# Layer 0 of a graph network: one-hot products among half-array ones as two of 64 columns, lists loaded by SP, a pause before each fetched block

## The chip, the cores and the metric

The kernel runs on one core of a Trainium2 chip. The core has a matrix engine (TensorE, PE in the profile; its weight loads are PEld), a vector engine (VectorE, DVE), a scalar engine (ScalarE, ACT), a general engine (GpSimd, POOL), and a sequencer that issues transfers (SyncE, SP), beside 16 DMA engines that all queues share. Each engine works through its own instructions in order and waits on semaphores for the others. The metric is the device time of one execution in microseconds, lower is better.

## The reference

The input is a graph of 12500 nodes with 64 features and 212500 directed edges, sorted by their receiving node (`dst`), each with 64 features of its own. What is computed, cut to what matters:

```python
h = maximum(layernorm(x), 0)
for i in range(3):                                   # layers 0, 1, 2
    agg = segment_sum(h[src], dst) / maximum(count(dst), 1)
    h = agg @ Wl[i] + h @ Wr[i] + b[i]               # relu after all but the last
x = x + h
h = maximum(layernorm(x), 0)
agg = segment_sum(edge_attr, dst) / maximum(count(dst), 1)
y = relu(concat(agg, h) @ W0 + b0); y = relu(y @ W1 + b1)
out = x + y @ W2 + b2
```

## The kernel before

Nodes stand in 98 blocks of 128. The sum over the edges of a node is computed in two ways.

**Dense blocks (78 of 98, in 20 groups of four, the last of two).** For each group the kernel builds a matrix of counts, 12544 x 512 bytes of fp8: how often each source node sends to each receiver. A layer multiplies the rows of h with it. The rows stand as three bf16 parts side by side (3 x 64 columns), whose sum is the f32 value. `Layer.group` does it in two streams of 98 products with 512 moving columns each: `whole` (line 392) takes two of the parts as 128 columns of the array; `half` (line 403) takes the third part as 64 columns, even blocks of nodes into the lower half of the array's columns and of the accumulator's partitions, odd ones into the upper. `Weave.run` orders them: 56 whole products, 56 half ones, the other 42 whole ones, the other 42 half ones.

**Fetched blocks (the first 20 of 98).** Here each block takes 19 x 128 edges in order. For each 128 edges GpSimd gathers the rows of h by an indirect DMA (`fetch`, line 461, tile `got`, eight tiles, so eight fetches ahead), and one product of 128 columns with a one-hot matrix of the receivers' places (`own`, made by VectorE in `mark`) adds them up in the accumulator `pg` (`use`, line 489). Two blocks share one accumulator; VectorE reduces it into `ga` (line 496) before the next two may use it. `use(i)` also requests fetch i + 8.

**Weave.** All other work is hung between these streams. `wide(pos, fn)` puts a function behind the whole product number `pos` of a layer (1960 of them, the position); `narrow(pos, sub, fn)` puts one behind half product `sub` of a group. `spread` places the 380 products of the fetched blocks at positions `spot(i, first)`: evenly spaced from `first` (220, 90 and 60 in layers 0, 1 and 2) to 90 before the end.

**Layer 0 also builds the matrices.** During the stream of group t, matrix t + 1 is built. VectorE makes one-hot operands (`h` with L790 and L791, `c` with L792) in batches of 8 or 10 of them; `pair` (line 809) multiplies two of them into an accumulator `pb`, 128 columns with 245 moving, and ScalarE casts that to the matrix (L812). There are three such accumulators. Of the 26 pairs of two blocks, or 52 of a group, 40 stand at positions among the whole products and 12 are `narrow`, two at a time, at half products 6, 20, 34, 48, 62 and 76. SP stores each half of a matrix to DRAM when its last cast is done (line 834); layers 1 and 2 load them back.

What goes into the one-hots comes from `index(j, box)`: a search for the first edge of each node of four blocks. It is a chain over the engines, each step hung at an offset: ScalarE counts the heads of tiles that lie before the node (0), GpSimd gathers the tile of 512 receivers, `ends` (7), ScalarE counts in it, `inside` (29), VectorE works out the edge and GpSimd gathers 128 receivers and senders from there, `to` and `of` (36, line 567), and so on. `coded(t)` hangs that for matrix t at 15 before the end of a group. `listed(j)` does the same for the five sets of four fetched blocks, and appends `lists(j)`: eight gathers on GpSimd, two for each block (108 and 120), of the receivers and senders of its 19 x 128 edges, then VectorE's working-out of places and rows (150). It begins 255 positions before the set's first product (205 for the first set).

The orders on TensorE, VectorE, ScalarE and GpSimd are those of the code; SP's follows a scheduler. In layers 1 and 2 SP also loads blocks of edge features: `load` reads the first edge into a register (`values_load`) and issues a plain load from there.

Of the kernel before, what the change touches and what calls it, by code (L numbers as in the profile page):

```python
# [11 lines left out]
F32 = mybir.dt.float32  # L12
I32 = mybir.dt.int32
# [6 lines left out]
ALU = mybir.AluOpType  # L20
# [9 lines left out]
P = 128  # L30
# [41 lines left out]
def in_order(  # L72
# [196 lines left out]
    class Carved:  # L269
# [6 lines left out]
        def tile(self, shape, dtype, name, bufs=None):  # L276
            size = 1
            for k in shape[1:]:
                size *= k
            if name not in self.places:  # L280
                self.places[name] = self.at
                self.at += self.bufs * size
            k = self.uses[name] = self.uses.get(name, -1) + 1
            o = self.places[name] + k % self.bufs * size
            t = self.t[: shape[0], o : o + size]
            return t if len(shape) == 2 else t.rearrange("p (a d) -> p a d", d=shape[2])
# [7 lines left out]
    class Weave:  # L294
# [2 lines left out]

        def __init__(self):
            self.w, self.seq, self.wides, self.narrows = 0, 0, [], []

        def wide(self, pos, fn):
            self.seq += 1
# [6 lines left out]
        def run(self, whole, half):  # L309


            half = enumerate(half)
            for n in (TURN, None):
                for _ in islice(whole, n):
                    self.w += 1
                    while self.wides and self.wides[0][0] <= self.w:
                        heapq.heappop(self.wides)[2]()
                for i, _ in islice(half, n):
                    due = [f for f in self.narrows if f[0] <= i and f[1] <= self.w]
                    for f in sorted(due):  # L320
                        self.narrows.remove(f)
                        f[3]()
                    heapq.heapify(self.narrows)

        def rest(self):
            while self.wides or self.narrows:
# [29 lines left out]
    class Layer:  # L356
# [122 lines left out]
        def use(self, i):  # L479
            b, k = divmod(i, EK)  # L480
            if i == 0:
                self.mark(0, 0)
            if i % (2 * EK) == 0:
                self.pg = self.psg.tile([P, 2, 3 * D], F32, name="pg")
            if i % (4 * EK) == 0:
                self.ga = self.pool.tile([P, 4, D], F32, name="ga", bufs=2)
            if k % QE == 0:
                self.mark(b, k // QE + 1)
            nc.tensor.matmul(  # L489
                self.pg[:, b % 2, :], self.owned.pop(i), self.fetched.pop(i),  # L490
                start=k == 0, stop=k == EK - 1,
            )
            self.fetch(i + NGOT)
            if k + 1 < EK:
                return
            nc.vector.tensor_reduce(  # L496
                self.ga[:, b % 4, :],
                self.pg[:, b % 2, :].rearrange("p (i d) -> p d i", i=3), axis=AX.X, op=ALU.add,
            )
            if b % 4 == 3:  # L500
                ga, j0, w = self.ga, b - 3, self.weave
                box = {}

                def sums():
                    pt = self.psc.tile([D, 4, P], F32, name="pt")
                    for k in range(4):
                        nc.tensor.transpose(pt[:, k, :], ga[:, k, :], ident)
                    box["agg"] = self.pool.tile([D, 4 * P], F32, name="gat", bufs=1)
                    nc.scalar.copy(box["agg"], pt.rearrange("p k n -> p (k n)"))

                def own_rows():
                    ht = self.turn(j0, 4)
                    w.wide(w.w + 9, lambda: self.mix(box["agg"], ht, j0, 4, inv_u))

                w.narrow(w.w + 1, 40, sums)
                w.narrow(w.w + 1, 68, own_rows)

    steps = NB * len(dense_groups)

    def spot(i, first):  # L520

        return first + i * (steps - first - 90) / (EK * GB)

    def spread(layer, first):
        for i in range(EK * GB):
# [18 lines left out]
    with ExitStack() as s:  # L544
# [27 lines left out]
        def index(j, box):  # L572
# [17 lines left out]
            def ends():  # L590

                box["tile"] = tile("tile_of", 1)
                nc.vector.tensor_scalar(
                    box["tile"], box["s"], -0.5, 1.0 - TT / 2, op0=ALU.mult, op1=ALU.max
                )
                tile_i = tile("tile_i", 1, I32)
                nc.vector.tensor_scalar(tile_i, box["tile"], TT / 2 - 1.0, None, op0=ALU.add)
                box["ends"] = tile("ends", TW, I32)
                gather(box["ends"], tiles_d, tile_i[:, :1])

            def inside():
# [130 lines left out]
        def lists(j):  # L732

            box = {}

            def edges(k0):
                if k0 == 0:
                    box["of"] = idx.tile([P, 4, EK], I32, name="l_of")
                    box["to"] = idx.tile([P, 4, EK], I32, name="l_to")
                for k in (k0, k0 + 1):  # L740
                    b = 4 * j + k
                    gather(box["to"][:, k, :], dst, mine[:, b : b + 1])
                    gather(box["of"][:, k, :], src, mine[:, b : b + 1])

            def places():
                for k in range(4):
                    b = 4 * j + k
                    nc.vector.tensor_scalar(
                        place[:, b], box["to"][:, k, :, None].to_broadcast([P, EK, 2]),
                        float(b * P), None, op0=ALU.subtract,  # L750
                    )
                lo = idx.tile([P, 4, EK], I32, name="l_lo")
                nc.vector.tensor_scalar(lo, box["of"], P - 1, None, op0=ALU.bitwise_and)
                hi = idx.tile([P, 4, EK], I32, name="l_hi")
                nc.vector.tensor_scalar(hi, box["of"], 7, None, op0=ALU.logical_shift_right)
                nc.vector.scalar_tensor_tensor(
                    rows_of[:, 4 * j : 4 * j + 4, :], lo, float(NB), hi, op0=ALU.mult, op1=ALU.add
                )

            return [(108, lambda: edges(0)), (120, lambda: edges(2)), (150, places)]  # L760
# [38 lines left out]
        def build(m, t, n):  # L799


            def pair(block, q):
                for i, (t_, k, q0, _) in enumerate(batches):
                    if (t_, k, q0) == (t, block, q):
                        hots(i + 1 + AHEAD)
                pb = ps_b.tile([P, 2, 256], F32, name="pb")
                for i in range(2):
                    h, c = ready.pop((t, block, q + i))
                    nc.tensor.matmul(pb[:, i, : HP * WD], h, c, start=True, stop=True)  # L809
                k = WD if q < Q5 else WD - 1  # L810
                o = P * (block % 2) + WD * q - max(q - Q5, 0)
                nc.scalar.copy(  # L812
                    m[:, block // 2, :, o : o + 2 * k].rearrange("p h (w d) -> p h w d", d=k),
                    pb[:, :, : HP * WD].rearrange("p w (h d) -> p h w d", d=WD)[:, :, :, :k],
                )

            return [
                lambda b=b, q=q: pair(b, q) for b in range(n) for q in range(0, QW, 2)
            ]
# [103 lines left out]
        with tc.manual_schedule(engines={PE, DVE, ACT, POOL}):  # L923
# [34 lines left out]
                    w.wide(at + a, f)  # L958

            for j in range(GB // 4):  # L960
                steps_at(spot(4 * EK * j, FIRST) - (255 if j else 205), listed(j))
            w.wide(FIRST - 50, layer.fetch_first)
            spread(layer, FIRST)
            steps_at(1 - 15, coded(2))
# [55 lines left out]
    def load(b):  # L1020
        if b is None:
            return

        n = EK * P
        raw = ed.tile([P, n // P * D + 1], F32, name="raw")
        first = raw[:1, n // P * D :].bitcast(I32)
        nc.vector.tensor_scalar(first, mine[:1, b : b + 1], float(EP - n), None, op0=ALU.min)
        at0 = nc.values_load(
            first, engines=[SP], min_val=0, max_val=EP - n,
            skip_runtime_bounds_check_because="it is clamped, and is not under 0",  # L1030
        )
        raw = raw[:, : n // P * D].rearrange("p (k d) -> p k d", d=D)
        nc.sync.dma_start(raw, edge[ds(at0, n), :].rearrange("(p k) d -> p k d", k=EK))
        if b < GB:
            box[b] = raw, place[:, b]
            return
        to = ed.tile([P, EK], I32, name="e_to")
        nc.sync.dma_start(to, dst[ds(at0, n), :].rearrange("(p k) o -> p (k o)", k=EK))
        at = ed.tile([P, EK, 2], BF16, name="e_at")
        nc.vector.tensor_scalar(  # L1040
            at, to[:, :, None].to_broadcast([P, EK, 2]), float(b * P), None, op0=ALU.subtract
        )
        box[b] = raw, at
# [734 lines left out]
```

## Time and profile before

| what | value |
|---|---|
| time, median of 3 runs (lowest to highest) | 2887.91 us (2884.1 to 2899.18) |
| the profiled execution, its time | 2895.6 us |
| its span, first to last instruction | 2893.7 us |
| mean clock granted to TensorE | 0.985 |
| setup, to the first product of group 0 | 0 to 94 us |
| layer 0 | 94 to 1124 us |
| layer 1 | 1124 to 1876 us |
| layer 2 with edge sums and the last perceptron | 1876 us to the end |
| L392, L403 (whole, half products) | 1960 of each in each layer |
| L809 (one-hot products of the build) | 2028, all before 1091 us |
| L489 (products of fetched blocks) | 380 in each layer |

Layers are told apart by the first and the last of their products on L392. The time of a run includes some 2 us around the span. A product's duration in the profile is longer than its share of the stream, since products are pipelined: L392 has a mean of 378 ns, but one begins 0.216 us after the other. What a product costs is therefore read from one start to the next.

### The profile page before, as it was taken

To read this page: it belongs to the slowest core of one execution; us is meant where nothing else is said; L and a number is where in the kernel's file an instruction comes from. 1 tells how busy PE (TensorE), PEld (TensorE's weight loads), DVE (VectorE), ACT (ScalarE), POOL (GpSimd) and SP (SyncE) were. 2 spreads that over 40 slices of the span, in tenths; PEclk is the share of its full clock that TensorE was granted. 3 is DMA by queue.
4 is the path that set the end of the run, shared out by engine and by line. 5 is a ranking of instruction groups with operands and counts; after the bars stand their busy time and mean duration, and the time that the engine had idled before them with its cause. 6 is when DMAs were issued, how large, how long until landed. Compare 5 with 4: busy or idle time off the path is not lost.

```text
span 2893.7 us, 50078 instructions
## 1 busy us (share of the span) xinstructions
PE 2749.0 (95%) x19505; PEld 1600.9 (55%) x19505; DVE 1630.9 (56%) x3376; ACT 1122.5 (39%) x2339; POOL 1429.8 (49%) x1313
## 2 busy tenths in 40 slices
PE   1699999999999998999999999999999999999997
PEld 0455555555555554555555555655656565565655
DVE  8878788788788771211111111166666566666663
ACT  4666566666666661100000000033333333434332
POOL 5345667667575640555555555244444344444440
PEclk9999999999999998999999999999999999999998
DMA  3334434444444346766656665577667676667661
GB/s 97 160 128 169 154 137 169 169 164 149 160 167 156 138 158 224 236 212 210 208 190 205 210 212 191 191 232 238 218 200 226 195 231 216 203 219 232 207 211 36
DMA packets 203194, 537.43 MB, mean 186 GB/s; under 512 B 83874, under 2 KB 92195, under 8 KB 197955
## 3 DMA queue, kind: packets, MB, share of 16 engines
q1 hardware_dynamic: 143890, 458.08, 44.2%
q0 software_dynamic: 41360, 66.33, 10.2%
q10 hardware_dynamic: 17696, 9.74, 1.1%
q8 instruction: 154, 2.52, 0.4%
q14 instruction: 94, 0.76, 0.1%
HBM read 391.11 MB, written 142.90 MB: 185 GB/s over the span
## 4 chain that ended last, share of the span: by engine, by line
PE 83%; DVE 12%; DMA 3%; issue 1%; ACT 1%; POOL 0%; SPq 0%; ACTq 0%; DVEq 0%; POOLq 0%
PE p L392 39%; PE p L403 21%; PE pb L809 6%; PE pe L1138 5%; PE pg L489 3%; DVE c L792 3%; PE po L436 3%; PE po L440 3%; DVE h L790 2%; PE pt L425 2%; DVE h L791 1%; PE pm L1177 1%; PE pm L1186 1%; DMA ends<-in_dst_dram,tile_i 1%; DMA e_to<-in_dst_dram 1%
## 5 line engine op out<-in xcount | busy, mean ns | idle before, releaser
L461 POOL DMA_INDIRECT got<-h_d,rows_of x1140 | 1244.2, 1091 | 1246.0 <-PE pg L489 881.0
L812 ACT CAST m<-pb 128x490 uint16<-128x490 f32 (+1 forms) x1014 | 545.7, 564 | 329.1 <-PE pb L809 318.4
L392 PE MATMUL p<-m,rows 128*128 128x512 fp8e3 (+1 forms) x1960 | 569.6, 378 | 0.8 <-ACT m L812 0.8
L392 PEld LDWEIGHTS <-rows 128*128 128x128 bf16 x3920 | 374.6, 100 | 245.6 <-issue 45.9
L392 PE MATMUL p<-t,rows 128*128 128x512 fp8e3 (+1 forms) x1960 | 491.8, 378 | 0.9 <-ACT rows L263 0.9
L392 PE MATMUL p<-t,m 128*128 128x512 fp8e3 (+1 forms) x1960 | 458.4, 376 | 0.0
L809 PE MATMUL pb<-c,h 128*128 128x245 bf16 x2028 | 371.2, 276 | 57.0 <-ACT m L812 42.0
L336 DVE TENSOR_TENSOR own<-iota_l,place 128x640 bf16<-128x640 bf16 (+3 forms) x280 | 144.2, 516 | 360.2 <-PE pg L489 337.0
L403 PEld LDWEIGHTS <-rows 128*64 128x64 bf16 x3920 | 224.9, 110 | 217.5 <-issue 79.1
L809 PEld LDWEIGHTS <-h 128*128 128x128 bf16 x2028 | 190.9, 99 | 263.4 <-issue 105.5
L792 DVE TENSOR_TENSOR c<-iota_c,col 128x1968 bf16<-128x1968 bf16 (+1 forms) x234 | 298.6, 1276 | 0.0
L489 PE MATMUL pg<-got,own 128*128 128x192 bf16 x1140 | 281.7, 247 | 15.7 <-DVE ga L496 8.3
L392 PEld LDWEIGHTS <-m 128*128 128x128 bf16 x1960 | 184.7, 99 | 184.0 <-issue 13.9
L403 PE MATMUL p<-m,rows 128*64 128x512 fp8e3 (+1 forms) x1960 | 254.1, 378 | 0.0
L403 PE MATMUL p<-t,rows 128*64 128x512 fp8e3 (+1 forms) x1960 | 252.0, 377 | 0.0
L1052 ACT CAST cut<-raw 128x640 bf16<-128x640 f32 x196 | 136.5, 697 | 247.7 <-PE pe L1138 221.6
L790 DVE TENSOR_TENSOR h<-iota_l,lo 128x1024 bf16<-128x1024 bf16 (+1 forms) x234 | 173.6, 742 | 94.9 <-PE pb L809 94.4
L403 PE MATMUL p<-t,m 128*64 128x512 fp8e3 (+1 forms) x1960 | 225.5, 375 | 0.0
L1054 ACT CAST cut<-e_rest 128x640 bf16<-128x640 f32 x196 | 136.8, 698 | 221.5 <-DVE e_rest L1053 220.5
L1055 DVE TENSOR_TENSOR cut<-e_rest,cut 128x640 bf16<-128x640 f32 x196 | 154.8, 790 | 81.9 <-ACT cut L1054 81.4
L1138 PE MATMUL pe<-cut,own 128*128 128x192 bf16 x1862 | 188.3, 248 | 0.0
L1138 PEld LDWEIGHTS <-own 128*128 128x128 bf16 x1862 | 161.6, 99 | 40.5 <-issue 2.9
(189 smaller groups left out, 2566.1 us busy)
## 6 DMA issues: line engine op xcount, KB each, us to landing
t<-mat SPq DMA_DIRECT2D x546, 448.0 KB, 5.9
mat<-m SPq DMA_DIRECT2D x39, 3136.0 KB, 9.9
raw<-in_edge_dram SPq DMA_DIRECT2D x98, 608.0 KB, 4.1
got<-h_d,rows_of POOLq DMA_INDIRECT x1140
h_d<-rows SPq DMA_DIRECT2D x14, 336.0 KB, 2.2
h_d<-rows ACTq DMA_DIRECT2D x24, 192.0 KB, 2.5
h_d<-out SPq DMA_DIRECT2D x21, 192.0 KB, 1.9
m<-h_d SPq DMA_DIRECT2D x6, 576.0 KB
```

The lines of the kernel that those rows point to most:

```text
L336: nc.vector.tensor_tensor(t[:, :n].rearrange("p k (c t) -> p k c t", t=2), iota_l.rearrange("p (c t) -> p c t", t=2)[:, None].to_broadcast ...
L392: nc.tensor.matmul(p1, rows[:, i, : 2 * D], at(i), start=i == 0, stop=i == NB - 1)
L403: nc.tensor.matmul(p2[h], rows[:, i, 2 * D :], at(i), start=i < 2, stop=i >= NB - 2)
L461: nc.gpsimd.indirect_dma_start(out=t, out_offset=None, in_=h_rows[self.l], in_offset=bass.IndirectOffsetOnAxis(ap=rows_of[:, b, k : k + 1] ...
L489: nc.tensor.matmul(self.pg[:, b % 2, :], self.owned.pop(i), self.fetched.pop(i), start=k == 0, stop=k == EK - 1,)
L790: nc.vector.tensor_tensor(split(th), pairs(iota_l, P), own(lo, P), op=ALU.is_equal)
L792: nc.vector.tensor_tensor(split(tc_), pairs(iota_c, CW), own(col, CW), op=ALU.is_equal)
L809: nc.tensor.matmul(pb[:, i, : HP * WD], h, c, start=True, stop=True)
L812: nc.scalar.copy(m[:, block // 2, :, o : o + 2 * k].rearrange("p h (w d) -> p h w d", d=k), pb[:, :, : HP * WD].rearrange("p w (h d) -> p ...
L1054: nc.scalar.copy(c[:, :, D : 2 * D], rest)
L1055: nc.vector.tensor_tensor(c[:, :, 2 * D :], rest, c[:, :, D : 2 * D], op=ALU.subtract)
L1138: nc.tensor.matmul(box["pe"], o[:, k - k0, :], c[:, k - k0, :], start=k == 0, stop=k == EK - 1)
```

## The change

Three things change.

1. `Weave` keeps a flag `halved`, which is true while half products are issued. A new method `product` issues a product as two of 64 columns each, with the same moving operand, into the lower and the upper 64 partitions of the accumulator, while the flag is true, and as one of 128 otherwise. `use` and `pair` issue theirs through it. Functions hung by `wide` run while the flag is false, so it is the 12 pairs of each of 19 matrices hung by `narrow` that are split: 456 products become 912. Layers 1 and 2 have none.
2. The lists of the fetched blocks no longer go by gathers on GpSimd. VectorE clamps the first edges of four blocks (`l_at`), SP reads each into a register, and two plain loads of 128 x 19 words fetch receivers and senders. The `ends` tile of `index` has one buffer instead of two. `first_of` and `in_block` are the shared helpers; `load` of the edge features uses them too and does what it did.
3. `spot` places the gathered products by 21 slots for each block of 19, the first two of them empty. This holds for all three layers. `listed(0)` begins 215 instead of 205 before its first product.

```diff
@@ class Weave
+            self.halved = False
...
             for n in (TURN, None):
+                self.halved = False
                 for _ in islice(whole, n):
                     self.w += 1
...
+                self.halved = True
                 for i, _ in islice(half, n):
...
+            self.halved = False
+
+        def product(self, out, lhsT, rhs, start, stop):
+
+            for h in (slice(0, D), slice(D, P)) if self.halved else (slice(0, P),):
+                nc.tensor.matmul(out[h], lhsT[:, h], rhs, start=start, stop=stop)
@@ Layer.use
-            nc.tensor.matmul(
+            self.weave.product(
                 self.pg[:, b % 2, :], self.owned.pop(i), self.fetched.pop(i),
-                start=k == 0, stop=k == EK - 1,
+                k == 0, k == EK - 1,
             )
@@
+    def first_of(at):
+        return nc.values_load(
+            at, engines=[SP], min_val=0, max_val=EP - EK * P,
+            skip_runtime_bounds_check_because="it is clamped, and is not under 0",
+        )
+
+    def in_block(table, at0):
+        return table[ds(at0, EK * P), :].rearrange("(p k) d -> p (k d)", k=EK)
+
     def spot(i, first):
 
-        return first + i * (steps - first - 90) / (EK * GB)
+        b, k = divmod(i, EK)
+        return first + (b * (EK + 2) + k + 2) * (steps - first - 90) / ((EK + 2) * GB)
@@ index
-                box["ends"] = tile("ends", TW, I32)
+                box["ends"] = tile("ends", TW, I32, 1)
                 gather(box["ends"], tiles_d, tile_i[:, :1])
@@ lists
                     box["to"] = idx.tile([P, 4, EK], I32, name="l_to")
+                    box["at"] = idx.tile([1, 4], I32, name="l_at", bufs=2)
+                    nc.vector.tensor_scalar(
+                        box["at"], mine[:1, 4 * j : 4 * j + 4], float(EP - EK * P), None,
+                        op0=ALU.min,
+                    )
                 for k in (k0, k0 + 1):
-                    b = 4 * j + k
-                    gather(box["to"][:, k, :], dst, mine[:, b : b + 1])
-                    gather(box["of"][:, k, :], src, mine[:, b : b + 1])
+                    at0 = first_of(box["at"][:, k : k + 1])
+                    for to, ends in ((box["to"], dst), (box["of"], src)):
+                        nc.sync.dma_start(to[:, k, :], in_block(ends, at0))
@@ pair
-                    nc.tensor.matmul(pb[:, i, : HP * WD], h, c, start=True, stop=True)
+                    layer.weave.product(pb[:, i, : HP * WD], h, c, True, True)
@@
-                steps_at(spot(4 * EK * j, FIRST) - (255 if j else 205), listed(j))
+                steps_at(spot(4 * EK * j, FIRST) - (255 if j else 215), listed(j))
```

More of the change, by code (lines that the diff above doesn't have):

```diff
@@ L1022, in load @@
             return
[L1024 to L1033, printed above, removed]
+        raw = ed.tile([P, EK * D + 1], F32, name="raw")
+        first = raw[:1, EK * D :].bitcast(I32)
+        nc.vector.tensor_scalar(first, mine[:1, b : b + 1], float(EP - EK * P), None, op0=ALU.min)
+        at0 = first_of(first)
+        nc.sync.dma_start(raw[:, : EK * D], in_block(edge, at0))
+        raw = raw[:, : EK * D].rearrange("p (k d) -> p k d", d=D)
         if b < GB:
@@ L1037, in load @@
         to = ed.tile([P, EK], I32, name="e_to")
[L1038 removed]
+        nc.sync.dma_start(to, in_block(dst, at0))
         at = ed.tile([P, EK, 2], BF16, name="e_at")
```

## The prediction

> **What bounds the kernel now.** I read the page's head and the table of slices first, then the busy time of each engine by layer, then TensorE's waits in layer 0, then the timeline of one group of layer 0, and last the waits of GpSimd there.
>
> ```profile
> span 2893.7 us, 50078 instructions
> PE 2749.0 (95%) x19505; PEld 1600.9 (55%) x19505; DVE 1630.9 (56%) x3376; ACT 1122.5 (39%) x2339; POOL 1429.8 (49%) x1313
> DVE  8878788788788771211111111166666566666663
> PE 83%; DVE 12%; DMA 3%; issue 1%; ACT 1%; POOL 0%; SPq 0%; ACTq 0%; DVEq 0%; POOLq 0%
> ```
>
> TensorE (PE) is busy 95% of the span and carries 83% of the chain that ended last. The slices of VectorE (DVE) show where another engine comes near: the first 15 or so, layer 0, at eight tenths. By layer (columns: stretch, its length, busy of PE, PEld, DVE, ACT, POOL with instruction counts, clock, DMA share, GB/s):
>
> ```profile
> 94.00:1124.00 1030.00, 994.33 (x7075) 578.97 (x7074) 802.30 (x1652) 645.23 (x1457) 593.34 (x494) 0.99 0.44 161
> 1124.00:1876.00 752.00, 741.05 (x5063) 406.26 (x5063) 110.93 (x253) 54.25 (x108) 363.06 (x380) 0.99 0.63 207
> 1876.00:2894.00 1018.00, 996.98 (x7303) 606.19 (x7297) 632.74 (x1275) 376.99 (x663) 425.12 (x380) 0.98 0.65 205
> ```
>
> In layer 0 VectorE still has 1030 - 802 = 228 us idle and GpSimd 437 us, so a shorter TensorE stream there shortens the layer. What TensorE loses to waits in layer 0 (total us, times, longest) is little:
>
> ```profile
> PE po L436 <- DVE e L409: 11.7, 13, 3.9
> PE pb L809 <- ACT m L812: 11.0, 12, 5.6
> PE pg L489 <- DVE ga L496: 5.1, 4, 2.0
> PE pg L489 <- DVE own L336: 3.1, 1, 3.1
> PE pg L489 <- DMA got<-h_d,rows_of: 3.1, 2, 1.6
> ```
>
> A larger loss is no wait. The timeline around 401 us (start, length, instruction, count) shows half-array products (128*64, L403) with one-hot products (128*128, L809) among them:
>
> ```profile
> 401.26 0.84 PE L403 MATMUL p<-m,rows 128*64 128x512 fp8e3 x6
> 402.03 0.60 PE L809 MATMUL pb<-c,h 128*128 128x245 bf16 x4
> 402.56 0.84 PE L403 MATMUL p<-m,rows 128*64 128x512 fp8e3 x6
> ...
> 405.40 2.56 PE L403 MATMUL p<-m,rows 128*64 128x512 fp8e3 x21
> ```
>
> The 21 products at 405.40 are ten and a half pairs in 2.56 us: a pair takes 0.216 us, as its second half starts 0.004 us after the first in the records of the trace. So three pairs from 401.26 should end streaming at 401.91, but L809 starts at 402.03; four products at 0.105 should take 0.42 us, but L403 is back only after 0.53. Over all 114 such places (19 matrices x 6, four products each) the trace gives, in medians: last pair to first L809 0.312 us, first to last L809 0.329, last L809 to next pair 0.199, and the first pair after it lasts 0.240 in place of 0.216. On average 0.839 + 0.024 = 0.863 us, of which streaming is 0.216 + 4 x 0.105 = 0.636. That the width makes the price and not the change of line: L403 to L392 (64 to 128 columns) shows the same 0.312, while L809 to L489 (both 128) shows 0.109 and L403 to L425 (both 64) no gap at all.
>
> **The change, part by part.** (1) The 456 products of these places go as two of 64 columns. If the halves overlap as the pairs of L403 do, a place takes 0.216 + 0.004 + 4 x 0.1065 = 0.646 us. 0.1065 lies between 0.1045 (streaming 245 columns) and 0.112 (two weight loads of 64 columns one after another: on L425 each product, with such a load of its own, follows the last by 0.056). Gain 0.863 - 0.646 = 0.217 us, times 114: **-24.8 us**; ends -25.5 and -22.3. Below that stands only a rival (no overlap: 0.210 a product). ACT's casts (L812, 0.564 us) get 1.93 us instead of 2.15 for two, so three accumulators still cover them.
>
> [...]
>
> (2) The slots of the gathered products (L489) move: every block gets 21 slots for 19 products, two of them empty before its first. A pair of blocks shares one accumulator (pg), so its first product waits for the reduction of the two before: 5.1 us in layer 0 above and 3.2 in layer 2 (the same row there), longest 2.0. The pause at a block's start grows from 4.3 positions (a position is one L392 product; in layer 0, with the work among them, 0.37 us) to 11.8, from 1.6 to 4.3 us, past the longest wait. Of 8.3 I take **-7.5**; ends 0 and -8.3.
>
> Slots stand 10% closer otherwise, which eats into the lead of the fetches: GpSimd issues one per 1.245 us at best, and in layer 1 products follow each other by 0.95 to 1.16 us. Lead from issue to use there is now 6.9 us at least; replayed with the new slots it falls by 1.2 to 1.5, to about 5.5. Landings in layer 1: median 3.0 us, 95% under 6.0, longest 7.1. **+0.5**; ends 0 and +5.
>
> (3) The lists go from 40 GpSimd gathers to 40 SP loads and 20 register reads. On GpSimd they held back the fetches in bursts of four (5 us); the smallest leads of layer 0 (4.7 to 6.4 us) stand behind them, and so do both waits for got, 3.1 us, and one stall of 1.5 us at 680 us, where ACT waited for a landing of 12 us. **-4**; ends 0 and -4.6. SP's own waits in layer 0 are for ACT's casts ahead of the matrix stores (665.7 us, mere idleness). The list loads stand behind stores of 3136 KB that land in 9.9 us, and each waits for the eighth DMA before it; their like, e_to, lands in 4.0 us, at most 9.1. They have 30 positions, 11 us, until VectorE wants them; without that cover VectorE would stand, as it does now for 7.3 us in all. The stores behind the register reads have a whole group (51 us). Five minima on VectorE, at most 0.19 us each, vanish in its idle time.
>
> (4) The "ends" list has one buffer instead of two. An index's gather of it stands at +7 and its reading on ACT at +29, so a gather that falls between another's two must wait on GpSimd, and all fetches behind it. By the formulas this happens once: list 3 starts at 962.9 (gather 969.9, reading 991.9) and the code of group 12 at 965 (gather 972). GpSimd then stands about 20 positions and 42 half-array products, 10 to 12 us, near 600 us. Such a stand is covered by eight fetched blocks today:
>
> ```profile
> POOL to L567 <- DVE at_i L614: 21.3, 6, 12.9
> POOL ends L567 <- ACT m L812: 20.3, 7, 13.1
> ```
>
> But here it owes, once free, seven fetches, the gather, and four more gathers of both indices: 12 x 1.245 = 15 us, while the fetch requested behind them is wanted 15 us after, and lands 3 us later (8.0 at the 95th of a hundred in layer 0, when a matrix store runs beside it). Replaying layer 0 with these times gives 5.2 to 8.4 us of waiting near 620 us; ACT also waits 2.3 us for the late landing, of which three accumulators hide half. **+7.5**; ends 0 and +11.
>
> (5) VectorE's adds ahead of po (11.7 us, 13 times) come later against a faster TensorE: **+2**; ends 0 and +11.7 (doubled).
>
> Sum: -24.8 - 7.5 + 0.5 - 4 + 7.5 + 2 = **-26.3 us**. The profiled execution took 2895.6 us (span 2893.7), which becomes 2869.3; it stands 7.7 us above the median of 2887.91, so the forecast is **2861.6 us**, 0.9% faster. All good ends give 2849.5, all bad ones 2893; six bad ends would have to meet for that, so I take this case to reach from 2849.5 to 2875. Under 0.5% (14.4 us) a measurement of this kernel can't be told from no change.
>
> **The rivals.** *An issue price of its own for each product.* For it: the 4-column products of L673 never stand closer than 0.025 us. Against: L403. 456 x 0.025 = 11.4 us back: 2873.
>
> *Fetches become the bound.* For it: (4), and closer slots in layers 0 and 1 with landings of up to 11.3 us beside a matrix store. Against: only two waits for got in the whole trace. If the stand near 600 us costs twice as much and layer 1 waits 5 us: about 2877.
>
> *The halves do not overlap.* Two products on the same bf16 columns, with waits on ACT ahead of them, are not seen side by side in this trace: L403 pairs read an fp8 operand. Then a place takes 0.22 + 8 x 0.105 = 1.06 us, 0.2 more than now: +22.5 instead of -24.8, 2909 and slower. It decides from 0.162 us a product.
>
> *The switch does not go away* (the gap belongs to the bank or to the semaphore, not to the width). Against: the transitions above. Then only (2) to (5) are left, -1.5: 2886.
>
> **How the numbers follow.** Forecast 0.64, issue price 0.10, fetches 0.11, no overlap 0.10, switch stays 0.05. Faster by over 0.5%: the forecast but 0.01, half of the issue price, 0.04 of the fetches: 0.72. Slower: no overlap and 0.02 from tails: 0.12. The rest, 0.16, is within. The range starts at 2848, just under all good ends, and goes up past the fetches to 2884; left out are no overlap, most of "switch stays" and a few tails.
>
> **What would show it.** (1) In the timeline of a group, four pairs of 128*64 at about 0.106 us a product among L403, no pause of 0.1 us on either side; 0.21 a product is the third rival, 0.13 the first. (2) The row of waits for ga is gone in layers 0 and 2. (3) No list gathers on GpSimd; VectorE's wait for the lists is under 10 us. (4) One stand of GpSimd of over 10 us before an "ends" near 590 us, then waits for got of 5 to 8 us. (5) po's wait for e stays under 15 us. Wrong it would be if VectorE's waits in layer 0 grew by what TensorE saves, or if layer 1, where nothing of (1) is, grew longer than 752 us.

## The result, and the profile after

The changed kernel takes 2881.05 us in the median (2876.22 to 2886.72, 20 runs), the kernel before 2891.3 us (2882.59 to 2902.09, 20 runs beside them). The ratio is 0.9963 [0.9953, 0.9973]: 0.37% faster, some 10.7 us. That is a real gain, but under the 0.5% that the prediction had set as what can be told from no change, and less than half of the 26.3 us forecast. The profiled execution took 2884.42 us, 11.2 us less than the one of before.

The head of the page and its chain, after:

```profile
span 2882.6 us, 51079 instructions
PE 2727.4 (95%) x19961; PEld 1642.7 (57%) x19961; DVE 1628.5 (56%) x3381; ACT 1122.3 (39%) x2339; POOL 1377.5 (48%) x1273
PE 83%; DVE 12%; DMA 2%; issue 2%; ACT 1%; POOL 0%; SPq 0%; ACTq 0%; DVEq 0%; POOLq 0%
```

The 456 new products are there and TensorE (PE) is still what bounds the kernel. By layer, after (stretch, its length, busy of PE, PEld, DVE, ACT, POOL, clock, DMA share, GB/s):

```profile
94.00:1116.00 1022.00, 973.72 (x7530) 620.78 (x7530) 800.87 (x1657) 644.42 (x1456) 542.21 (x454) 0.97 0.44 162
1116.00:1868.00 752.00, 740.88 (x5057) 405.68 (x5056) 110.86 (x253) 54.01 (x108) 362.98 (x380) 0.99 0.62 207
```

Layer 0 is 8 us shorter, layer 1 is as long as before; the other 3.5 us were saved in layer 2. The reader should see one column that the prediction did not speak of: the clock in layer 0 went from 0.99 to 0.97. Splitting layer 0 by the four stretches of its 20 groups (from the first product of each stretch to the first of the next, summed) says where the gain was and where it went:

| stretch | before, us | after, us | difference |
|---|---|---|---|
| 56 whole products | 440.5 | 463.2 | +22.7 |
| 56 half products | 188.3 | 167.9 | -20.4 |
| 42 whole | 281.1 | 279.1 | -2.0 |
| 42 half | 125.6 | 117.5 | -8.1 |

The half stretches, where the split is, gave 28.5 us. The stretch that opens the next group, where no instruction of TensorE was split, took 22.7 us back. What TensorE waits for in layer 0, after (total us, times, longest):

```profile
PE po L446 <- DVE e L419: 23.8, 15, 4.0
PE pb L333 <- ACT m L839: 13.0, 12, 5.6
PE pg L333 <- DMA got<-h_d,rows_of: 3.8, 3, 3.3
PE pt L517 <- DVE ga L506: 2.4, 1, 2.4
```

The first row is the same wait that had 11.7 us and 13 times before (line numbers have moved: L446 was L436, L419 was L409, and `product`, now L333, stands for L489 and L809). `po` is the small product of a group's finished sum with the layer's weights (`mix`), hung five positions into the next group; `e` is the sum of the two accumulators, for which VectorE (DVE) does the last addition after the half stretch. One such place near 884 us, first on TensorE (start, length, engine, line, operation, tiles, shape, count, the wait before it):

```profile
883.12 0.38 PE L402 MATMUL p<-m,rows 128*128 128x512 fp8e3 x1
885.39 0.43 PE L446 MATMUL po<-wl,e 128*128 128x64 f32 x2 [1.89 <-DVE e L419]
885.66 0.55 PE L450 MATMUL po<-wr,ht 65*128 65x64 f32 x2
886.00 0.63 PE L446 MATMUL po<-wl,e 128*128 128x64 f32 x2
886.43 0.63 PE L450 MATMUL po<-wr,ht 65*128 65x64 f32 x2
```

And on VectorE at the same time:

```profile
879.81 0.68 DVE L817 TENSOR_TENSOR h<-iota_l,lo 128x1024 bf16<-128x1024 bf16 x1
880.53 0.69 DVE L818 TENSOR_TENSOR h<-h,weight 128x1024 bf16<-128x1024 bf16 x1
881.14 1.18 DVE L819 TENSOR_TENSOR c<-iota_c,col 128x1968 bf16<-128x1968 bf16 x1
882.23 0.68 DVE L817 TENSOR_TENSOR h<-iota_l,lo 128x1024 bf16<-128x1024 bf16 x1
882.95 0.69 DVE L818 TENSOR_TENSOR h<-h,weight 128x1024 bf16<-128x1024 bf16 x1
883.56 1.18 DVE L819 TENSOR_TENSOR c<-iota_c,col 128x1968 bf16<-128x1968 bf16 x1
884.65 0.68 DVE L419 TENSOR_TENSOR e<-e,p 128x512 f32<-128x512 f32 x1
```

VectorE is not idle: it makes one-hot operands for the next matrix, two batches of 2.4 us without a pause, and the addition of `e` waits in its queue behind them until 884.65. TensorE comes to the end of its half stretch earlier than before, VectorE does not, and TensorE stands for 1.89 us. Over 19 groups, the addition begins 2.58 us behind the last half product in the mean, 1.85 us before. The second part shows in TensorE's rows above, where the pairs after 885.66 take 0.43 us each, and in four windows around the place (stretch, length, PE, PEld, DVE, ACT, POOL, clock, DMA, GB/s):

```profile
850.00:883.00 33.00, 33.00 (x284) 20.95 (x282) 29.20 (x67) 22.42 (x52) 22.13 (x17) 1.00 0.47 164
883.00:885.70 2.70, 0.81 (x7) 0.42 (x5) 2.33 (x3) 0.74 (x2) 1.11 (x1) 1.00 1.04 446
885.70:892.50 6.80, 6.80 (x28) 4.68 (x27) 0.84 (x2) 1.14 (x2) 0.94 (x1) 0.50 0.45 184
892.50:900.00 7.50, 7.50 (x50) 4.69 (x49) 6.90 (x13) 5.95 (x13) 5.50 (x5) 1.00 0.13 26
```

For 6.8 us after the pause TensorE was granted half its clock: 28 products where the 7.5 us behind them have 50. In such stretches the whole products start 0.427 us apart instead of 0.216. It looks fully busy there, so no row of waits shows the loss. From the trace's record of the clock, layer 0 had 20.5 us at half clock before and 58.0 us after. They come in stretches of 3.413 us, or two or three of those. Of the 16 stretches of both traces, 13 begin 2.4 to 4.8 us after the start of a pause of at least 1.3 us (start to start), and three (two before, one after, 3.413 us each) begin without a pause, behind a set of small products. Not every such pause is followed by one; the last section says which. By the products inside them, 10.5 us of streaming were lost before and 28.7 us after. The lower clock is not this one execution's: in the 20 runs of the changed kernel the mean granted clock was 0.977 to 0.983, 0.980 in the median; the kernel before had 0.985 in the median of the 23 runs that stand beside the first experiments. As an estimate from these means, the median run lost some 14 us to the clock, a little less than the profiled one.

So two sums can be set beside the +22.7 us: start to start, the pauses before `po` went from 13.5 us (12) to 25.9 us (14), +12.4, and the half clock cost 18.2 us more. Together they are 30.6 us, more than the stretch lost; the other way went the waits for `ga` ahead of `pg` in this layer (5.1 us before, none after) and most of that for `own` (3.1, now 1.0). The last of the four rows, `pt`, the transposition of `ga` (L517), which waits 2.4 us for `ga`, is new; it belongs to the slots and comes up again below.

### The profile page after: what moved, and what is told of

The parts are those of the page before. It is cut to its first block, busy times and chain, and to the rows that moved or that the text cites. A ratio compares the mean times of both kernels' runs of the same rounds, so it can differ in the third digit from the quotient of the medians.

```text
span 2882.6 us, 51079 instructions
## 1 busy us (share of the span) xinstructions
PE 2727.4 (95%) x19961; PEld 1642.7 (57%) x19961; DVE 1628.5 (56%) x3381; ACT 1122.3 (39%) x2339; POOL 1377.5 (48%) x1273
## 3 DMA queue, kind: packets, MB, share of 16 engines
q1 hardware_dynamic: 149650, 458.47, 44.4%
## 4 chain that ended last, share of the span: by engine, by line
PE 83%; DVE 12%; DMA 2%; issue 2%; ACT 1%; POOL 0%; SPq 0%; ACTq 0%; DVEq 0%; POOLq 0%
PE p L402 39%; PE p L413 20%; PE pb L333 5%; PE pe L1160 5%; DVE c L819 3%; PE pg L333 3%; PE po L446 3%; PE po L450 3%; DVE h L817 2%; PE pt L435 2%; DVE h L818 1%; PE pm L1199 1%; PE pm L1208 1%; DMA ends<-in_dst_dram,tile_i 1%; DMA after<-in_dst_dram 1%
## 5 line engine op out<-in xcount | busy, mean ns | idle before, releaser
L402 PE MATMUL p<-m,rows 128*128 128x512 fp8e3 (+1 forms) x1960 | 575.8, 381 | 0.8 <-ACT m L839 0.8
L333 PE MATMUL pb<-c,h 128*128 128x245 bf16 (+1 forms) x2484 | 394.5, 275 | 60.9 <-ACT m L839 44.7
L346 DVE TENSOR_TENSOR own<-iota_l,place 128x640 bf16<-128x640 bf16 (+2 forms) x280 | 144.0, 516 | 390.9 <-PE pg L333 363.0
L333 PEld LDWEIGHTS <-h 128*128 128x128 bf16 (+1 forms) x2484 | 229.4, 104 | 232.0 <-issue 67.0
L413 PEld LDWEIGHTS <-rows 128*64 128x64 bf16 x3920 | 255.2, 109 | 185.0 <-issue 53.7
L333 PE MATMUL pg<-got,own 128*128 128x192 bf16 x1140 | 281.8, 247 | 4.8 <-DMA got<-h_d,rows_of 3.8
L413 PE MATMUL p<-m,rows 128*64 128x512 fp8e3 (+1 forms) x1960 | 266.5, 376 | 0.0
L413 PE MATMUL p<-t,rows 128*64 128x512 fp8e3 (+1 forms) x1960 | 250.7, 376 | 0.0
L413 PE MATMUL p<-t,m 128*64 128x512 fp8e3 (+1 forms) x1960 | 225.5, 375 | 0.0
```

The lines of the kernel that those rows point to most:

```text
L333: nc.tensor.matmul(out[h], lhsT[:, h], rhs, start=start, stop=stop)
L346: nc.vector.tensor_tensor(t[:, :n].rearrange("p k (c t) -> p k c t", t=2), iota_l.rearrange("p (c t) -> p c t", t=2)[:, None].to_broadcast ...
L402: nc.tensor.matmul(p1, rows[:, i, : 2 * D], at(i), start=i == 0, stop=i == NB - 1)
L413: nc.tensor.matmul(p2[h], rows[:, i, 2 * D :], at(i), start=i < 2, stop=i >= NB - 2)
```

## Experiments

In the expectations G says that a gap in front of `po` costs itself and the clock behind it, so that the split's gain goes there; V, that VectorE has become the bound, so that a wait taken away at `po` comes back elsewhere; C, that the clock falls for a reason of its own, gap or no gap. The first four, the next four and the last four ran on one chip each; the kernel before had medians of 2893.55, 2968.47 and 2893.08 us there, and kernels are compared within a chip.

**The changed kernel, with `mix` nine positions later in layer 0.** The data that `po` needs are the same, it only asks later, behind nine more products that are ready anyway.

```diff
-            w.wide(w.w + 5, lambda: self.mix(box["e"], box["ht"], j0, n, inv))
+            w.wide(w.w + self.mix_at, lambda: self.mix(box["e"], box["ht"], j0, n, inv))
@@ the loop over the groups of layer 0
+                layer.mix_at = 14 if t + 1 < len(order) else 5
```

> The changed kernel with one number changed: in layer 0 the po products of a dense group stand 14 instead of 5 positions into the next group (all but the last group). Theory G (given back): the split shortens the half-array stretches of layer 0 by 28 us as forecast, but VectorE's add ahead of po comes no earlier, TensorE waits there (24 us against 12), and after such a pause the granted clock drops to half for 3.4 us or more (58 us of it in layer 0 against 20). With VectorE given 9 positions more, waits for e in layer 0 fall under 5 us, half clock under 30 us, and the time by 22 to 35 us against the changed kernel, to 2846 to 2860. Rival V (VectorE or ScalarE is the bound of layer 0): the wait turns up elsewhere, at pb or at the next p, and the time stays within 6 us of the changed kernel's. Rival C (the clock drops because of the 64-column products, not because of pauses): half clock in layer 0 stays at 45 us or more, and the gain is at most 15 us.

2845.29 us, 0.9826 [0.9804, 0.9848]. Layer 0 in a window of its own, then TensorE's waits there:

```profile
94.00:1078.00 984.00, 957.52 (x7537) 613.87 (x7538) 801.64 (x1657) 648.81 (x1457) 536.39 (x454) 0.99 0.47 168
```

```profile
PE pb L333 <- ACT m L840: 13.3, 12, 5.6
PE pg L333 <- DMA got<-h_d,rows_of: 4.9, 2, 4.5
PE po L447 <- DVE e L420: 1.1, 1, 1.1
```

The wait went from 23.8 to 1.1 us and did not come back in another row, VectorE is as busy as before in a layer that is 38 us shorter, and the clock is back at 0.99. V falls: VectorE had the time, only not at that moment. Its addition is even as late as it was (2.57 us behind the last half product in the mean); `po` only no longer asks for it then. The half clock in layer 0 fell from 58.0 to 23.9 us. The stretch of 56 whole products went from 463.2 to 422.7 us, and the half stretches kept what the split had given (169.7 and 117.5). Pauses gone (25.9 - 1.3 = 24.6 us) and half of the half-clock time gone (17 us) are 41.6 us; layer 0 became 38.7 us shorter.

**The kernel before, with the same move.** The gap existed before too, so moving `po` must be worth something there; what counts is how much less.

> The kernel before with the same one number: po 14 instead of 5 positions into the next group in layer 0. Theory G: it has 12 us of waits for e in layer 0 and 20 us of half clock, so it gains 10 to 20 us against the kernel before. Rival V: nothing, within 5 us of the kernel before. If this gains as much as the first run against the changed kernel, the change itself has no part in the loss.

2879.13 us, 0.9940 [0.9917, 0.9964]: the move alone gives some 17 us on the kernel before. Its pauses at `po` went (1.3 us left), its half clock did not fall in the profiled execution (34.1 us, 20.5 in the one of before). Pauses are not the reason: 27.3 of the 34.1 us begin behind the four sets of small products of the gathered blocks (`po<-wl,gat`, 16 f32 products of 64 moving columns in 2.9 us), without a pause. The windows around one set, TensorE busy throughout:

```profile
398.90:402.40 3.50, 3.50 (x21) 2.67 (x21) 0.50 (x2) 0.57 (x1) 0.17 (x1) 1.00 0.90 351
402.40:412.60 10.20, 10.20 (x40) 6.85 (x39) 5.42 (x11) 3.73 (x8) 3.04 (x4) 0.50 0.08 21
```

With `po` out of the way in both, the change is worth 0.9826 / 0.9940 = 0.9885, 33 us, where the changed kernel itself showed 10.7. The gain was made, and the gap took two thirds of it.

**The split alone**, on the kernel before: `product` for the pairs of the build, nothing else (the flag and the method, as in the change, are left out here).

```diff
-                    nc.tensor.matmul(pb[:, i, : HP * WD], h, c, start=True, stop=True)
+                    layer.weave.product(pb[:, i, : HP * WD], h, c, True, True)
```

> The kernel before with the split alone (slots and lists as before). Theory G: half-array stretches of layer 0 shorter by 24 to 30 us; waits for e up by 5 to 12 us and half clock up by 15 to 40 us against the kernel before; net gain 0 to 12 us. Rival C: the same half clock with no more waits than before. If the split were worth its 25 us by itself, 2864 to 2868.

2885.36 us, 0.9972 [0.9957, 0.9987]. The half stretches are 32.9 us shorter than before (167.7 and 113.3), the whole ones 22.8 us longer (455.0 and 289.4). Two of its rows of waits in layer 0:

```profile
PE po L446 <- DVE e L419: 22.6, 16, 3.9
PE pg L499 <- DVE ga L506: 3.8, 4, 1.1
```

So it is the split that doubles the wait at `po`; half clock 44.4 us.

**Everything but the split**: the changed kernel with `halved` kept false.

```diff
-                self.halved = True
+                self.halved = False
```

> The changed kernel without the split (all one-hot products 128 columns wide; slots and lists as changed). Theory G: half-array stretches as long as before, waits for e in layer 0 back near 12 us and half clock near 20 to 30 us; the time is that of slots and lists alone, 5 to 11 us under the kernel before. Rival C: half clock falls to 20 us as well, so this run does not tell C apart; it tells whether slots and lists by themselves bring waits (then half clock stays over 40 us).

2897.72 us, 1.0012 [1.0000, 1.0023]. Half stretches as before (189.3 and 127.8). Its waits in layer 0:

```profile
PE po L446 <- DVE e L419: 14.4, 12, 3.9
PE pg L333 <- DMA got<-h_d,rows_of: 5.8, 1, 5.8
```

The slots and the lists without the split give nothing: the wait for a fetched block (`got`) is the one that step (4) had placed, and the half clock rose to 37.5 us.

**Pauses without any split.** The changed kernel, where VectorE in layer 1, which has no split product, multiplies `e` by one four times after its addition, so that `po` is late there.

```diff
                     nc.vector.tensor_tensor(box["e"], box["e"], p2, op=ALU.add)
+                    for _ in range(4 if self.l == 1 else 0):
+                        nc.vector.tensor_scalar(box["e"], box["e"], 1.0, None, op0=ALU.mult)
```

> The changed kernel with four more VectorE operations in each group of layer 1, behind the add that po waits for, each a multiplication of e by one: they leave out nothing and only delay po, by a pause of some 1 to 2 us in each of 20 groups of a layer in which TensorE never waits otherwise and no product is split. If pauses drop the clock: half clock in layer 1 rises from 20 us to over 45 us, each episode 2 to 4 us behind a pause, and layer 1 grows by the pauses and half of the added half clock. If it is the 64-column products or layer 0's mix of work that drops it: half clock in layer 1 stays near 20 us, and layer 1 grows by the pauses alone.

3020.11 us, 1.0163 [1.0133, 1.0193], on the chip where the kernel before took 2968.47. Waits of TensorE in its layer 1, then the layer, one stretch at half clock and one at full:

```profile
PE po L448 <- DVE e L421: 33.4, 19, 3.2
PE p L413 <- issue: 20.1, 39, 1.2
```

```profile
1160.00:2018.00 858.00, 791.75 (x5020) 421.26 (x5018) 144.16 (x329) 53.09 (x106) 363.28 (x380) 0.94 0.53 182
1388.40:1402.10 13.70, 13.70 (x44) 8.06 (x44) 3.21 (x8) 1.64 (x4) 3.25 (x4) 0.50 0.35 127
1410.00:1430.00 20.00, 20.00 (x149) 10.61 (x150) 0.92 (x2) 0.58 (x1) 9.89 (x11) 1.00 0.62 210
```

19 pauses of some 1.9 us each were made, and 13 were followed by half clock, 2.7 to 4.8 us after their start; the layer has 95.6 us of it (23.9 in the run below). The layer took 858.2 us against 772.6 to 793.5 us in the other three kernels on this chip: 33 us are the pauses, and about half of the added 72 us the clock. C falls as far as pauses are concerned: VectorE's pauses bring the low clock, in a layer without one split product. On this chip TensorE also has pauses for which the profile names no releaser (the second row, "issue"): before half products in layer 1 and before one-hot products in layer 0, and next to none in layer 2. Why is left open; in the traces of the kernels before and after, and in those of the split alone and of the fastest kernel, there is none.

**Step (4) taken away.** The first kernel of this section, with list 3 begun 22 positions earlier, so that its `ends` doesn't stand across that of the matrix code.

```diff
-                steps_at(spot(4 * EK * j, FIRST) - (255 if j else 215), listed(j))
+                steps_at(spot(4 * EK * j, FIRST) - {0: 215, 3: 277}.get(j, 255), listed(j))
```

> As the first run (po 14 positions into the next group in layer 0), and the index of the fourth list of fetched blocks begins 277 instead of 255 positions ahead, so that no gather of the one-buffered ends tile falls between another's gather and its reading. Step (4) of the prediction: the pauses near 600 us (2.6 us at pb, 4.9 us at got, 6.8 us of half clock, in the first run's trace) go; 7 to 11 us under the first run, 2834 to 2838. Rival (the lists moved by SP are what is late there): the pauses stay, within 3 us of the first run.

> The fifth run again: on its chip TensorE stood in all three layers for pauses whose releaser the profile does not show (up to 1.5 us each, 43 of them in layer 1 alone), and the kernel before took 2968 us instead of 2891, so its distance to the first run could not be read. On a chip without them: ratio to the kernel before 0.978 to 0.981 (the first run had 0.9826), no wait for got and no pause at pb near 600 us. Rival: the ratio is that of the first run within 0.002, and other pauses stand in the place of these.

On the second chip (e7) 2923.55 us, 0.9844 [0.9816, 0.9873]; on the third (f1) 2832.37 us, **0.9788 [0.9768, 0.9808]**: the fastest kernel of all, 2.1% under the kernel before, some 60 us. Its layer 0 and what TensorE waits for there, on the third chip:

```profile
94.00:1070.00 976.00, 958.27 (x7585) 615.50 (x7584) 801.87 (x1657) 648.81 (x1459) 536.87 (x454) 0.99 0.47 170
```

```profile
PE pb L333 <- ACT m L840: 8.9, 7, 5.6
PE po L447 <- DVE e L420: 1.1, 1, 1.1
PE pg L333 <- DMA got<-h_d,rows_of: 0.4, 1, 0.4
```

Layer 0 is 13 us shorter than with list 3 where it was; the waits near 600 us (2.6 us before a `pb`, 4.9 for a `got`, and 6.8 us of half clock behind) are gone. The two traces are of different chips.

**The same, with the slots even as before** (`spot` as in the kernel before; the second list begins 247 instead of 255 positions ahead, the others as in the run beside it).

> As the run beside it (split, lists by SP, po 14 positions into the next group, ends overlaps moved apart), but with the slots evenly spaced as in the kernel before. Prediction's step (2): without the pause ahead of each block the waits for ga come back, 8 us in layers 0 and 2, so 5 to 10 us slower than the run beside it. Rival S (the new slots cost elsewhere what they save, as the changed kernel without the split hinted): within 4 us of it, or faster.

2839.07 us, 0.9817 [0.9803, 0.9830]: the slots are worth 6.7 us once the pauses are gone, by the intervals with some 7 us to either side. The row that they were to remove is back, in layer 0 and in layer 2:

```profile
PE pg L333 <- DVE ga L507: 3.0, 5, 0.9
...
PE pg L333 <- DVE ga L507: 3.1, 5, 1.5
```

**The slots alone**, on the kernel before (with the first list begun 10 positions earlier), twice:

```diff
-        return first + i * (steps - first - 90) / (EK * GB)
+        b, k = divmod(i, EK)
+        return first + (b * (EK + 2) + k + 2) * (steps - first - 90) / ((EK + 2) * GB)
```

> The kernel before with the new slots alone (and the first list 10 positions earlier, without which its rows would not be ready); lists by GpSimd, two ends buffers, products 128 wide. The changed kernel without the split came out 4 us slower than before; this run and the next say which half of it does that. Prediction's step (2): waits for ga gone in layers 0 and 2, -5 to -8 us, 2885 to 2889. Rival: the new slots bring pauses of their own in layer 0 (half clock over 30 us), and the time is that of before or above it.

> The sixth run again, slots alone on the kernel before, which was 0.6% slower on the other chip. Rival S: 0 to 10 us slower than before, with half clock in layer 0 over 30 us. Prediction's step (2): 5 to 8 us faster.

1.0059 [1.0040, 1.0078] on the second chip, 1.0006 [0.9994, 1.0019] on the third. In layer 0 of the trace from the third chip the wait at `po` is 15.1 us against 11.7 in the kernel before, the half clock 41 us against 20.5 (mean clock 0.983 in the median of its 12 runs, 0.986 in those of the kernel before), and `pt` waits 2.3 us for `ga`, which it did not do before. That these took what the slots gave is likely, but was not tested:

```profile
PE po L436 <- DVE e L409: 15.1, 12, 3.9
```

**The lists by SP and the one buffer alone**, twice: the changed kernel without split and with the old `spot`.

> The kernel before with the lists loaded by SP and one ends buffer alone (slots even, products 128 wide, first list 10 positions earlier). Two overlaps of the ends buffer remain here, of 6 and 12 positions. Prediction's steps (3) and (4) together: between -4 and +4 us of the kernel before; with the half clock that follows a pause, 0 to +8. Rival: SP's loads come late and VectorE stands for them, more than 10 us of such waits in layer 0.

> The seventh run again, lists by SP and one ends buffer alone on the kernel before, which was 1.0% faster on the other chip. If that holds here, 2862 to 2875 and the lists are worth far more than step (3) gave them; if the gain was that chip's, between -4 and +4 us of the kernel before.

0.9895 [0.9872, 0.9918] on the second chip, 0.9990 [0.9976, 1.0003] on the third, where its waits in layer 0 are

```profile
PE po L446 <- DVE e L419: 9.4, 13, 3.5
PE pg L333 <- DVE ga L506: 3.8, 4, 1.1
```

The two chips disagree on the slots and the lists by more than their intervals. The second is the one with the pauses of no known cause, and its figures for parts of a few us are not used. On the first and third chips the parts add up to what the change gives: split -0.28%, slots +0.06%, lists -0.10%, together -0.32% against the -0.37% measured. Each part has an interval of 0.13 to 0.15% to either side, and the slots and lists in one kernel gave +0.12%, so the sum fits but proves little.

## Why the prediction was wrong, point by point

**The bound** was read rightly: TensorE's stream in layer 0, with time to spare on VectorE. What was not weighed is that spare time on average does not say whether VectorE is free at the moment when `e` is due.

**(1) The split: -24.8 us forecast. Right.** The place near 398 us in the profile after:

```profile
397.74 0.84 PE L413 MATMUL p<-m,rows 128*64 128x512 fp8e3 x6
398.41 0.59 PE L333 MATMUL pb<-c,h 128*64 128x245 bf16 x8
398.83 0.81 PE L413 MATMUL p<-m,rows 128*64 128x512 fp8e3 x6
```

From the last pair of L413 (398.190) to the next (398.835) it takes 0.645 us, forecast 0.646. The four pairs of halves start 0.105, 0.109 and 0.108 us apart, the second half 4 ns after the first, and there is no pause on either side. Over the 114 places, ten half products and the four split ones between take 1.504 us in the median, 1.730 before: 0.226 us each, 25.8 in all. The half stretches shrank by 28.5 to 32.9 us; the few us over the places were not followed up. The rivals "halves do not overlap" and "the switch does not go away" are excluded by this, and so is an issue price: of the 25 ns for a second product, the least distance of the 4-column products on L673 in the trace of before, nothing is seen. In the trace of before a change of width costs time, about 0.22 us for the way there and back (1.730 us a place, 1.504 where the width stays).

**(2) The slots: -7.5 us. Right for the rows it named, hidden in the sum.** The rows for `ga` ahead of `pg` are gone in layers 0 and 2; in the fastest kernel the slots are worth some 6.7 us. What the sum lacked is a wait that they bring: `pt` stands for `ga` once in layer 0, 2.3 to 3.2 us in all eight kernels with the new slots and never in the six with even ones (0.7 us more in layer 2 of the changed kernel). So some 3 of the 8.3 us came back, and in the changed kernel 3.4 us of half clock follow that pause at 558.0 us. By themselves the slots gave nothing (1.0006). The closer slots cost no wait in layer 1, as taken.

**(3) The lists: -4 us. Right within what can be told.** No row of VectorE waits for the lists, and with one buffer for `ends` but without the new slots they gave 0.9990 [0.9976, 1.0003], some -2.9 us with 4 us to either side. GpSimd's stands for that buffer were 5.7 and 7.1 us there, and TensorE had no wait for `got`, so that figure goes beside the -4 and not beside -4 + 7.5.

**(4) The one buffer for `ends`: +7.5 us. Right in place, with a price that was too low.** GpSimd's waits from 560 to 680 us after, and TensorE's from 590 to 680 us:

```profile
POOL got L471 <- PE pg L333: 28.9, 13, 12.7
POOL ends L589 <- ACT signs L604: 14.8, 1, 14.8
```

```profile
PE pb L333 <- ACT m L839: 4.4, 3, 2.5
PE pg L333 <- DMA got<-h_d,rows_of: 3.3, 1, 3.3
PE po L446 <- DVE e L419: 2.4, 2, 1.3
```

One stand of 14.8 us ahead of `ends` (forecast 10 to 12), then waits at 627 (2.9 us between products) and 641 us. The wait for `got` itself is 3.3 us, under the 5.2 to 8.4 replayed, but half clock follows (3.4 us from 629.7). Taking it away gave 13.1 us in layer 0 between two kernels of different chips, of which the waits for `got` and `pb` and half of the half clock explain 11. That is the bad end of the step's range or beyond it.

**(5) "VectorE's adds ahead of po come later against a faster TensorE: +2 us." This is the step that failed.** The row went from 11.7 to 23.8 us. The end of its own range, +11.7 "(doubled)", was the true size; the price taken was near the other end, with no row for it. The rows were there: VectorE at eight tenths through layer 0 and with 2.4 us batches back to back at a group's end, and a wait that already came in 13 of 20 groups. Per group the split saves about 1.2 us ahead of `po`, all on TensorE, and VectorE's order and work stay what they were: its addition stands 0.73 us further behind the last half product in the mean (1.85 us before, 2.58 after). Over 19 groups that is some 14 us, and 12.1 us are what the row grew by.

**A term was missing: the clock.** The page before gave 0.985 as a mean and 0.99 in layer 0, and the sum took both for a constant. In the traces of before and after, 13 of the 16 stretches of half clock in layer 0 stand behind a pause of 1.3 us or more, and each cost another 1.7 us (half of 3.413) or two or three times that. In layer 0 the clock cost 18.2 us more than before. Forecast (5) plus clock +2, measured +12.4 + 18.2 = +30.6: 28.6 us too little. The whole sum was off by 15.1 us in the profiled executions, so the other steps did some 13 us better than forecast; how that divides between (1) to (4) and the scatter of the clock from one execution to the next was not separated.

What "would make it wrong" was named rightly in the prediction (VectorE's waits in layer 0 growing by what TensorE saves), but it had no chance or price of its own among the rivals.

## What to carry to other kernels

Where a faster stream ends in a product that already waits for another engine in most rounds, expect to lose much of the gain at that product until it asks later: here moving it by nine positions of ready work turned 0.9963 into 0.9826, and starting one list earlier made that 0.9788. An idle share of a fifth on the other engine is no cover; look at what stands in its queue ahead of the one instruction that is waited for. And price a pause on TensorE at more than its own length (here 12.4 us more of pauses before `po` stood beside 18.2 us more lost at half clock): read the granted clock in a window right behind it.

## What was not expected of the hardware

- Pauses of 1.3 to 2.9 us from one start to the next could be enough for half clock. In the layers 0 of the kernels before and after, eight of 28 such pauses were followed by it 2.4 to 3.7 us after their beginning, for 3.413 us or twice that (28 products in 6.8 us where 50 fit into 7.5). Before `po` it was six of 13, before other products two of 15. In layer 1 of the kernel with the four multiplications it was 13 of 19 pauses of about 1.9 us.
- What told one pause from the next in the traces of before and after was mostly its place. In each of the two all changes of the granted clock lie on one grid of 3.413 us, to within 1 ns. Of six pauses of 1.6 to 2.3 us ahead of `po` in their layers 0 (with no other pause over 0.6 us within 5.5 us), the four that began 0.1 to 0.9 us after a line of the grid were followed by half clock, and the two that began 1.3 and 1.9 us after one were not. It goes without a pause too: of the eight sets of 16 small products of gathered blocks in these layers, which take 2.9 us each, the three that began from 0.2 us before to 0.8 us after a line were followed by half clock, and the five that began elsewhere were not. The place doesn't settle every case: a pause of 1.47 us ahead of `po` at 244.88 us after the change began 0.9 us after a line and was not followed. Why the place counts was not worked out, and these are few cases.
- Two products of 64 columns on the same moving columns, each waiting for its own accumulator, ran beside each other as well as those that read an fp8 operand: after the change, from 398.4 us, 0.105 to 0.109 us a pair, the second 4 ns after the first. The two column halves even drifted apart: at 401 us one half of a matrix product starts 86 ns before the other half's last one-hot product.
- One chip of three had TensorE stand without a releaser, before half products in layer 1 (20.1 us, 39 times in one trace) and before one-hot products in layer 0, and ran the kernel before 2.6% slower. Parts worth a few us could not be told there.
